# Two layers of cross attention and expert FFNs on one core: column norms between the key products, 16-bit integers in the token lists, two operations moved to other engines

## The chip, the core and the metric

One Trainium2 chip, one of its cores. A core has TensorE (PE; its weight loads are shown apart as PEld), VectorE (DVE), ScalarE (ACT), GpSimd (POOL) and SyncE (SP, which issues DMAs here). The metric is the time of one execution on the device, in microseconds (us); lower is better.

## The reference, cut to what matters

Eight batches of 256 tokens of width 256, so 2048 tokens, go through four blocks, each added to its input after a layer norm. The change touches the first two blocks, and one bound that is worked out in them for the third.

```python
def _L0_xattn_ref(Q, K, V, Wq, bq, Wout, bout):          # block 1
    q = (Q @ Wq + bq).transpose(0, 2, 1)                 # width 16; K and V alike
    ...
    corr = jnp.real(jnp.fft.ifft(Qf * jnp.conj(Kf))).mean(axis=(0, 1))
    W_topk, I_topk = jax.lax.top_k(corr, K_TOP)          # 12 shifts
    W_topk = jax.nn.softmax(W_topk)
    ...                                                  # R: weighted rolls of v
    return R @ Wout + bout

def balanced_assignment(scores):                         # block 2
    for e in range(E):                                   # 8 experts, 256 tokens each
        s = jnp.where(taken, -jnp.inf, scores[:, e])
        _, idx = jax.lax.top_k(s, C)
        parts.append(idx)
        taken = taken.at[idx].set(True)
    return jnp.concatenate(parts)

def _L0_ffn_ref(x, centroids, ln_g, ln_b, w1, b1, w2, b2):
    scores = layer_norm(feat, ln_g, ln_b) @ centroids.T
    sort_by_expert = balanced_assignment(scores)
    routed = feat[sort_by_expert].reshape(E, C, D)
    h = layer_norm(routed, ln_g, ln_b)
    h = jax.nn.gelu(jnp.einsum('ecd,edf->ecf', h, w1) + b1[:, None, :])
    h = jnp.einsum('ecf,efd->ecd', h, w2) + b2[:, None, :]
    out = routed + h                                     # and back to token order

x = x + _L0_xattn_ref(_layernorm(x), ctx, ctx, ...)
x = x + _L0_ffn_ref(_layernorm(x), ...)
x = x + _L1_xattn_ref(_layernorm(x), ctx, ...)           # softmax attention, 16 heads
x = x + _L1_ffn_ref(_layernorm(x), ...)                  # top 2 of 8 gated experts, and shared ones
```

## The kernel before, in words

`fast_path` does all four blocks; `general_path` follows only where a flag says that a bound was broken. The order of instructions on each engine is written out by hand, and each engine executes its instructions in that order. What touches the change lies in the first 170 us:

1. Tokens and context are loaded, transposed and projected. The correlation of block 1 goes through memory (`Gd`, then `DG`), its maximum is taken (`pcorr`, L1757), the weights go through memory (`Wd`, then `CW`, L1787), and three short products follow: `pr3` (L1915), `pp` (L1927), and `PB`, which is spread to all tokens (`spread_rows`, L1850) on top of the tokens' own rows (`copy_rows`, L1836). Statistics of the sums, factors, and the scores `SC` follow up to 57 us.
2. While TensorE waits in this chain it is given steps of other work. `work` is a queue of such steps, and `fill(us)` takes steps from it until their written costs reach `us`; a step of 0.43 is one 128 x 256 product. First in the queue are the keys and values of block 3 (`keys`, L1391, and `vals`, L1412), which need nothing from block 1.
3. `column_norms` (L1374) sums the squares of the columns of Wq of block 3, four products with an output of one column; ACT scales them and POOL takes the root. They stand in slot 4 of the PSUM tile `pw`, among `small_products` (L1869, outputs of 32 columns).
4. Block 2 finds for each expert e a threshold with `search` (five rounds, L2198 to L2230: DVE counts tokens above a value, TensorE adds the counts up in `pcn`, L2215, DVE sets the next value). During the search for expert e the generator `list_tokens(e - 1)` is taken one step on after each round: `taken` and `sel` on DVE (L2253, L2257), `pse` on TensorE (L2262), `selt` and `before` on DVE, `ppl` on TensorE, `place`, `ab`, `oab`, `ob` on DVE (L2291 to L2300), `pid` (L2304) and `pix` (L2312) on TensorE, the token numbers `ids`, and two gathers of the tokens' rows `R` by POOL (L2323).
5. `ffn(e)` starts when the rows are there: ACT applies the layer norm (`R`, L2365), TensorE transposes (`turn_rows`, `prt`, L2385), ACT scales into `RT` (L2389), and 16 steps of `up` (`ph`, then a Gelu on ACT) and 16 of `down` (`py`, L2419) are appended to `work`. After each eight `down` steps DVE adds the bias `b2b` to `py` (L2428) and POOL scatters the 128 rows `Y` to memory (L2429). For experts 2, 3 and 4 `ffn` also copies a column of `blank` on ACT (L2374), and SP then stores blank rows to `Td` (L2376); the next expert's weights are loaded by SP too (L1813 to L1817).
6. SP's queue around 57 us is: the rows' stores to `NMd` (L2018, L2001), `SCd` (L2173), two loads of score rows (L2165), the stores of the factors (L1939), four more score rows, then the blanks `Yd` (L2178) and `Od` (L2182). The gathers of expert 0 need the rows and the factors in `NMd`.

Of the kernel before, what the change touches and what calls it, by code (L numbers as in the profile page):

```python
# [9 lines left out]
F32 = mybir.dt.float32  # L10
BF16 = mybir.dt.bfloat16
U32 = mybir.dt.uint32
I32 = mybir.dt.int32
AF = mybir.ActivationFunctionType
ALU = mybir.AluOpType
# [4 lines left out]
P = 128  # L20
# [1066 lines left out]
def fast_path(  # L1087
# [49 lines left out]
    NTB = T // TB  # L1137
    HW = 32
    F16 = mybir.dt.float16
    assert L0_xattn_Wq.shape[1] == DH and L1_ffn_w1_e.shape[2] == F  # L1140

    def tok_view(ap):
# [36 lines left out]
    def fill(us):  # L1179

        while work and us > 0.3:
            cost, do = work.popleft()
            do()
            us -= cost
# [185 lines left out]
    def column_norms(pn):  # L1370

        for c in range(NB):
            for kc in range(KC):
                nc.tensor.matmul(  # L1374
                    pn[:, c : c + 1],
                    wsq[:, kc, c * P : (c + 1) * P],
                    ones[:, 0:1],
                    start=(kc == 0),
                    stop=(kc == KC - 1),
                )  # L1380
        nc.scalar.activation(qmax, pn, AF.Copy, scale=257.0)
        nc.gpsimd.tensor_tensor(
            qmax, qmax, powers[:, 1:2].to_broadcast([P, NB]), ALU.pow
        )
        nc.gpsimd.tensor_tensor(qmax, qmax, babs, ALU.add)
# [230 lines left out]

    first = pr.tile([P, 4], BF16, name="first")
    nc.gpsimd.tensor_copy(first, ident.rearrange("p (g i) -> p g i", i=32)[:, :, 0])
    identb = pr.tile([P, P], BF16, name="identb")
    nc.gpsimd.tensor_copy(identb, ident)  # L1620
    onesb = pr.tile([P, P], BF16, name="onesb")
# [11 lines left out]
        channel_multiplier=-1,  # L1633
    )

    iab = pr.tile([P, NT, 2, 16], I32, name="iab")
    for j, base in enumerate((BASE // 16, 0)):
        nc.gpsimd.iota(
            iab[:, :, j, :],
# [103 lines left out]
    nc.tensor.transpose(pb1, b1r, ident[: E * NF, : E * NF])  # L1743
    b1c = pr.tile([P, E, NF], F32, name="b1c")
    nc.scalar.copy(b1c.rearrange("p e f -> p (e f)"), pb1)
    fill(4.3)
    nc.vector.scalar_tensor_tensor(tri, identb, float(BASE), tri, ALU.mult, ALU.add)
    ith = pa.tile([P, 1], F32, name="ith")
    nc.vector.tensor_reduce(ith, i32, AX.X, ALU.add)
# [84 lines left out]
    def copy_rows(b, pool, tag):  # L1834
        pos[b] = pool.tile([P, TPB, D], F32, tag=tag, name="po")
        nc.tensor.matmul(  # L1836
            pos[b].rearrange("p h d -> p (h d)"),
            ident,
            rows_of(b).rearrange("p h d -> p (h d)"),
            start=True,  # L1840
            stop=False,
            skip_group_check=True,
        )
# [17 lines left out]
    bdiag = pa.tile([E, E], F32, name="bdiag")  # L1861
    nc.vector.tensor_scalar(bdiag, ident[:E, :E], bnd, None, ALU.mult)
    WCn = pa.tile([P, 3, 32], F32, name="WCn")
    pw = ps_t.tile([P, 5, 32], F32, tag="pt", name="pw")
    pb = pw[:, 3, 0:E]

    def small_products(j):
        for dc in range(KC):
            nc.tensor.matmul(  # L1869
                pw[:, j, :],  # L1870
                wrt[:, dc, j * P : (j + 1) * P]
                if j < 2
                else boc[:, dc : dc + 1].to_broadcast([P, P]),
                cenP[:, dc, :],
                start=(dc == 0),
                stop=(dc == KC - 1),
            )

    copy_rows(order_b[0], ps_t, "pt")
    copy_rows(order_b[1], ps_t, "pt")  # L1880
    small_products(0)
    small_products(1)
    column_norms(pw[:, 4, 0:NB])
    copy_rows(order_b[2], ps_t, "pt")
    small_products(2)
    nc.tensor.matmul(pb, ones[:E, :], bdiag, start=True, stop=True)
    nc.vector.tensor_copy(WCn, pw[:, 0:3, :])
# [354 lines left out]
    def list_tokens(e, then):  # L2242

        if e == E - 1:

            sel = pm.tile([P, TB], BF16, tag="sel", name="sel")
            nc.vector.tensor_scalar(
                sel, taken[e - 1], -1.0, 1.0, ALU.mult, ALU.add
            )
        else:  # L2250
            n, thr = low[e]
            taken.append(pm.tile([P, TB], BF16, tag="taken", name="taken"))
            nc.vector.tensor_scalar(taken[e], n, thr, None, ALU.is_gt)  # L2253
            sel = taken[e]
            if e:
                sel = pm.tile([P, TB], BF16, tag="sel", name="sel")
                nc.vector.tensor_tensor(sel, taken[e], taken[e - 1], ALU.subtract)  # L2257
        yield

        pse = ps_t.tile([P, 4, 4], F32, tag="pt", name="pse")  # L2260
        for j in range(4):
            nc.tensor.matmul(  # L2262
                pse[:, j, :], sel[:, j * P : (j + 1) * P], first, start=True, stop=True
            )
        selt = pm.tile([P, NT], BF16, tag="selt", name="selt")
        nc.vector.tensor_scalar(
            selt.rearrange("p (g j) -> p j g", j=4),
            pse,
            1.0,
            None,  # L2270
            ALU.mult,
            ALU.add,
            accum_out=cnts[:, e : e + 1],
        )
        before = pm.tile([P, NT], BF16, tag="before", name="before")
        nc.vector.memset(before[:, 0:1], 0.0)
        nc.vector.tensor_tensor_scan(
            before[:, 1:],
            onesb[:, 0 : NT - 1],
            selt[:, 0 : NT - 1],  # L2280
            0.0,
            ALU.mult,
            ALU.add,
        )
        yield

        ppl = ps_t.tile([P, NT], F32, tag="pt", name="ppl")
        nc.tensor.matmul(ppl, tri, selt, start=True, stop=False)
        nc.tensor.matmul(ppl, onesb, before, start=False, stop=True)
        place = pm.tile([P, NT], I32, tag="place", name="place")  # L2290
        nc.vector.tensor_copy(place, ppl)  # L2291
        ab = pm.tile([P, NT, 2], I32, tag="ab", name="ab")
        nc.vector.tensor_scalar(ab[:, :, 0], place, 4, None, ALU.logical_shift_right)
        nc.vector.tensor_scalar(ab[:, :, 1], place, 15, None, ALU.bitwise_and)
        oab = pm.tile([P, NT, 2, 16], F16, tag="oab", name="oab")
        nc.vector.tensor_tensor(
            oab, ab.unsqueeze(3).to_broadcast([P, NT, 2, 16]), iab, ALU.is_equal
        )
        ob = pm.tile([P, NT, 16], F16, tag="ob", name="ob")
        nc.vector.tensor_tensor(ob, oab[:, :, 1, :], tok, ALU.mult)  # L2300
        yield
        pid = ps_t.tile([16, 16], F32, tag="pt", name="pid")
        for c in range(NT):
            nc.tensor.matmul(  # L2304
                pid, oab[:, c, 0, :], ob[:, c, :], start=(c == 0), stop=(c == NT - 1)
            )
        ids16 = pm.tile([16, 16], F16, tag="ids16", name="ids16")
        nc.vector.tensor_copy(ids16, pid)
        yield
        pix = ps_t.tile([P, NCT, 16], F32, tag="pt", name="pix")  # L2310
        for r in range(NCT):
            nc.tensor.matmul(  # L2312
                pix[:, r, :], rowsel[:, r, :], ids16, start=True, stop=True
            )
        m = pm.tile([P, NCT, 16], F32, tag="m", name="m")
        nc.vector.tensor_tensor(m, pix, bsel, ALU.mult)
        idf = pm.tile([P, NCT], F32, tag="idf", name="idf")
        nc.vector.tensor_reduce(idf, m, AX.X, ALU.add)
        ids = pm.tile([P, NCT], U32, tag="ids", name="ids", bufs=4)
        nc.vector.tensor_copy(ids, idf)  # L2320
        R = pf.tile([P, NCT, D + 2], F32, tag="R", name="R")
        for r in range(NCT):
            nc.gpsimd.indirect_dma_start(  # L2323
                out=R[:, r, :],
                out_offset=None,
                in_=NMd,
                in_offset=bass.IndirectOffsetOnAxis(ap=ids[:, r : r + 1], axis=0),
            )
        then(e, ids, R)
        if e == E - 1:  # L2330
            for r in range(NCT):
                nc.vector.tensor_scalar(
                    at0[:, r, :], row0, idf[:, r : r + 1], None, ALU.is_equal
                )
# [23 lines left out]
    def ffn(e, ids, R):  # L2358
# [57 lines left out]
        def down(r):  # L2416
            py = ps_k.tile([P, D], F32, tag="pm", name="py")
            for f in range(NF):
                nc.tensor.matmul(  # L2419
                    py,  # L2420
                    A[:, f, r * P : (r + 1) * P],
                    w2[:, f, :],
                    start=(f == 0),
                    stop=(f == NF - 1),
                )
                if f < NF - 1:
                    yield
            nc.vector.tensor_tensor(Y[:, r, :], py, b2b, ALU.add)  # L2428
            nc.gpsimd.indirect_dma_start(  # L2429
                out=Yd,  # L2430
                out_offset=bass.IndirectOffsetOnAxis(ap=ids[:, r : r + 1], axis=0),
                in_=Y[:, r, :],
                in_offset=None,
            )
            yield
# [1048 lines left out]
```

## Time and profile before

| what | us |
|---|---|
| median of 3 runs | 883.61 (883.28 to 885.3) |
| the profiled execution's own time | 878.66 |
| its span, first to last instruction | 876.9 |
| mean granted TensorE clock in it | 0.997 |
| DVE busy from 75 to 105 us of the span | 24.35 of 30 |
| ACT busy from 75 to 105 us | 14.70 of 30 |
| GpSimd busy from 75 to 105 us | 3.88 of 30 |
| TensorE busy from 105 to 155 us | 50.00 of 50 |

The profile's page gives busy time per engine and groups of instructions; the views by time (the timeline, and busy time by stretch) give each instruction's start in us from the span's start. A matmul on 32-bit data appears as two records, each with its own weight load; records overlap, so what one costs TensorE is the distance from its start to the next one's start, not its duration. "[1.38 <-DVE ob L2300]" behind a line says that the engine stood idle for 1.38 us before it, and what ended that.

### The profile page before, as it was taken

The numbers are of one execution on the slowest core, as the hardware profiler recorded it, in microseconds if no ns is written. First come the engines' busy times: TensorE is split into PE (matmuls) and PEld (weight loads), VectorE is DVE, ScalarE is ACT, GpSimd is POOL, SyncE is SP. The second block draws the span as 40 slices with busy tenths as digits, with TensorE's granted clock in tenths as the row PEclk, the third lists the DMA queues.
The fourth block names the chain that finished last, engine by engine and source line by source line (L and its number), as shares of the span: only waits on it lengthen the run. The fifth ranks groups of instructions, "written<-read, shape, count | busy, mean of one in ns | idle before, by whom it ended". The sixth has DMA issues, their size and how long they took to land. (4 is left out here: it accounts for less than half of the span.)

```text
span 876.9 us, 11147 instructions
## 1 busy us (share of the span) xinstructions
PE 856.0 (98%) x4180; PEld 533.7 (61%) x4180; DVE 308.8 (35%) x1017; ACT 266.2 (30%) x494; POOL 213.8 (24%) x298
## 2 busy tenths in 40 slices
PE   8999899999999999999999999999999999999997
PEld 6646688788455555545568474747464657474745
DVE  7377876412656765551111112020111111111021
ACT  4254443332677675321110111111111111111110
POOL 7161222302235464423310020201111131111200
PEclk9999999999999999999999999999999999999999
DMA  8475479840610001361211555565657434311130
GB/s 250 160 223 172 144 210 279 261 130 37 164 42 26 1 20 38 113 237 44 68 50 38 179 141 148 159 177 156 181 155 181 149 92 114 85 13 12 18 103 28
DMA packets 87126, 105.22 MB, mean 120 GB/s; under 512 B 8824, under 2 KB 77656, under 8 KB 87032
## 3 DMA queue, kind: packets, MB, share of 16 engines
q1 hardware_dynamic: 78520, 91.10, 32.9%
q0 software_dynamic: 7920, 13.02, 7.0%
q8 instruction: 35, 0.57, 0.3%
q10 hardware_dynamic: 624, 0.30, 0.1%
q14 instruction: 27, 0.22, 0.1%
HBM read 80.60 MB, written 25.37 MB: 121 GB/s over the span
## 5 line engine op out<-in xcount | busy, mean ns | idle before, releaser
L3113 DVE TENSOR_TENSOR A<-A,pu 128x512 f32<-128x512 f32 x96 | 66.0, 688 | 365.2 <-PE pu L3104 358.5
L3112 ACT ACTIVATE A<-pgt 128x512 f32<-128x512 f32 x96 | 57.3, 597 | 271.5 <-PE pgt L3104 271.5
L3173 POOL DMA_INDIRECT Od<-Y,ids x32 | 49.4, 1545 | 304.0 <-ACT Y L3186 213.3
L3104 PE MATMUL pgt<-RT,wa 128*128 128x512 f32 x256 | 121.2, 596 | 0.0
L3104 PE MATMUL pu<-RT,wb 128*128 128x512 f32 x256 | 120.3, 592 | 0.0
L3126 PE MATMUL py<-wc,A 128*128 128x256 f32 x512 | 111.8, 379 | 0.0
L3126 PEld LDWEIGHTS py<-wc,A 128*128 128x128 f32 x512 | 96.9, 190 | 13.1 <-issue 0.5
L3104 PEld LDWEIGHTS pu<-RT,wb 128*128 128x128 f32 x256 | 48.7, 190 | 61.1 <-issue 59.9
L2689 ACT ACTIVATE ex<-p,scale 128x512 f32<-128x512 f32 x128 | 77.2, 689 | 27.5 <-PE p L2681 26.3
L3104 PEld LDWEIGHTS pgt<-RT,wa 128*128 128x128 f32 x256 | 47.7, 190 | 54.8 <-issue 54.4
L2402 PE MATMUL ph<-RT,w 128*128 128x256 f32 x256 | 61.6, 390 | 1.5 <-ACT RT L2389 1.3
L2419 PE MATMUL py<-w,A 128*128 128x256 f32 x256 | 62.0, 389 | 0.0
L2402 PEld LDWEIGHTS ph<-RT,w 128*128 128x128 f32 x256 | 45.4, 190 | 9.9 <-ACT RT L2389 1.8
L2419 PEld LDWEIGHTS py<-w,A 128*128 128x128 f32 x256 | 46.6, 190 | 6.3
L2921 POOL DMA_INDIRECT Td<-HP,to x32 | 31.6, 988 | 63.3 <-DMA Td<-HP,to 60.3
L2411 ACT ACTIVATE A<-ph,b1c 128x256 f32<-128x256 f32 x64 | 30.0, 472 | 54.4 <-PE ph L2402 51.0
L3104 PE MATMUL pgt<-HT,wa_-1_2734 128*128 128x512 f32 x96 | 45.5, 597 | 0.0
L3104 PE MATMUL pu<-HT,wb_-1_2735 128*128 128x512 f32 x96 | 45.1, 593 | 0.0
L3186 ACT ACTIVATE Y<-py,R 128x256 f32<-128x256 f32 x32 | 15.2, 474 | 96.5 <-PE py L3126 96.5
L2681 PE MATMUL p<-QM,KT 32*128 32x512 f32 x256 | 43.4, 640 | 0.4 <-DVE QM L2662 0.4
L3126 PE MATMUL py<-wc_-1_2736,A 128*128 128x256 f32 x192 | 41.9, 379 | 0.0
L3126 PEld LDWEIGHTS py<-wc_-1_2736,A 128*128 128x128 f32 x192 | 36.5, 190 | 5.7 <-issue 1.0
(458 smaller groups left out, 984.8 us busy)
## 6 DMA issues: line engine op xcount, KB each, us to landing
w<-in_L_ffn_w_dram SPq DMA_DIRECT2D x16, 1024.0 KB, 7.3
wa<-in_L_ffn_w_e_dram SPq DMA_DIRECT2D x8, 1024.0 KB, 7.0
wb<-in_L_ffn_w_e_dram SPq DMA_DIRECT2D x8, 1024.0 KB, 8.7
wc<-in_L_ffn_w_e_dram SPq DMA_DIRECT2D x8, 1024.0 KB, 8.3
R<-Td SPq DMA_DIRECT2D x8, 530.0 KB, 7.2
sa<-in_L_ffn_w_e_dram SPq DMA_DIRECT2D x16, 256.0 KB, 4.2
sb<-in_L_ffn_w_e_dram SPq DMA_DIRECT2D x16, 256.0 KB, 4.8
sc<-in_L_ffn_w_e_dram SPq DMA_DIRECT2D x16, 256.0 KB, 5.7
```

What stands on the lines that cost most here:

```text
L2402: nc.tensor.matmul(ph, w1[:, kc, f * P : (f + 1) * P], RT[:, kc, :], start=(kc == 0), stop=(kc == KC - 1),)
L2411: nc.scalar.activation(A[:, f, :], ph, AF.Gelu_apprx_tanh, bias=b1c[:, e, f : f + 1])
L2419: nc.tensor.matmul(py, A[:, f, r * P : (r + 1) * P], w2[:, f, :], start=(f == 0), stop=(f == NF - 1),)
L2681: nc.tensor.matmul(ps[g].rearrange("p m q -> p (m q)"), KT[rows, c, k0 : k0 + P], QM[b][rows, c].rearrange("p m q -> p (m q)"), start=True ...
L2689: nc.scalar.activation(e4[:, g], ps[g], AF.Exp, scale=scale)
L2921: nc.gpsimd.indirect_dma_start(out=Td, out_offset=bass.IndirectOffsetOnAxis(ap=to[g][:, k, j : j + 1], axis=0), in_=HP[:, GT * g + j, :], ...
L3104: nc.tensor.matmul(ps, w_[:, kc, fs], xs[kc], start=(kc == 0), stop=(kc == KC - 1),)
L3112: nc.scalar.activation(a, pgt, AF.Silu)
L3113: nc.vector.tensor_tensor(a, a, pu, ALU.mult)
L3126: nc.tensor.matmul(py, A[:, f, s : s + P], wc[:, f, :], start=(f == 0), stop=(f == NF - 1))
L3173: nc.gpsimd.indirect_dma_start(out=Od, out_offset=bass.IndirectOffsetOnAxis(ap=ids, axis=0), in_=Y, in_offset=None, compute_op=ALU.add,)
L3186: nc.scalar.activation(Y, py, AF.Copy, scale=R[:, i, D + e : D + e + 1])
```

## The change

`column_norms` moves from between `small_products(1)` and the third `copy_rows` to the middle of the fill before `pcorr`, with a PSUM tile of its own; that fill is written as two of 1.73 instead of one of 4.3, and a fill of 0.86 stands after the third `copy_rows`. `small_products(0)` moves ahead of the second `copy_rows`. The integers `place`, `ab` and the constants `iab` become 16 bits wide. For experts 1, 2 and 3 the difference `sel` is no longer formed by DVE: `pse` adds the product of `taken[e]` with `first` and that of `taken[e - 1]` with its negative `nfirst` (a new constant made by POOL). For experts 0, 1 and 2 the bias is added in two operations, a copy out of PSUM by ACT and an addition by POOL, instead of one by DVE.

```diff
--- before.py
+++ after.py
@@ -1137,6 +1137,7 @@
     NTB = T // TB
     HW = 32
     F16 = mybir.dt.float16
+    I16 = mybir.dt.int16
     assert L0_xattn_Wq.shape[1] == DH and L1_ffn_w1_e.shape[2] == F
 
     def tok_view(ap):
@@ -1616,6 +1617,8 @@
 
     first = pr.tile([P, 4], BF16, name="first")
     nc.gpsimd.tensor_copy(first, ident.rearrange("p (g i) -> p g i", i=32)[:, :, 0])
+    nfirst = pr.tile([P, 4], BF16, name="nfirst")
+    nc.gpsimd.tensor_scalar(nfirst, first, -1.0, None, ALU.mult)
     identb = pr.tile([P, P], BF16, name="identb")
     nc.gpsimd.tensor_copy(identb, ident)
     onesb = pr.tile([P, P], BF16, name="onesb")
@@ -1633,7 +1636,7 @@
         channel_multiplier=-1,
     )
 
-    iab = pr.tile([P, NT, 2, 16], I32, name="iab")
+    iab = pr.tile([P, NT, 2, 16], I16, name="iab")
     for j, base in enumerate((BASE // 16, 0)):
         nc.gpsimd.iota(
             iab[:, :, j, :],
@@ -1743,7 +1746,9 @@
     nc.tensor.transpose(pb1, b1r, ident[: E * NF, : E * NF])
     b1c = pr.tile([P, E, NF], F32, name="b1c")
     nc.scalar.copy(b1c.rearrange("p e f -> p (e f)"), pb1)
-    fill(4.3)
+    fill(1.73)
+    column_norms(ps_t.tile([P, NB], F32, tag="pt", name="pn"))
+    fill(1.73)
     nc.vector.scalar_tensor_tensor(tri, identb, float(BASE), tri, ALU.mult, ALU.add)
     ith = pa.tile([P, 1], F32, name="ith")
     nc.vector.tensor_reduce(ith, i32, AX.X, ALU.add)
@@ -1861,7 +1866,7 @@
     bdiag = pa.tile([E, E], F32, name="bdiag")
     nc.vector.tensor_scalar(bdiag, ident[:E, :E], bnd, None, ALU.mult)
     WCn = pa.tile([P, 3, 32], F32, name="WCn")
-    pw = ps_t.tile([P, 5, 32], F32, tag="pt", name="pw")
+    pw = ps_t.tile([P, 4, 32], F32, tag="pt", name="pw")
     pb = pw[:, 3, 0:E]
 
     def small_products(j):
@@ -1877,11 +1882,11 @@
             )
 
     copy_rows(order_b[0], ps_t, "pt")
+    small_products(0)
     copy_rows(order_b[1], ps_t, "pt")
-    small_products(0)
     small_products(1)
-    column_norms(pw[:, 4, 0:NB])
     copy_rows(order_b[2], ps_t, "pt")
+    fill(0.86)
     small_products(2)
     nc.tensor.matmul(pb, ones[:E, :], bdiag, start=True, stop=True)
     nc.vector.tensor_copy(WCn, pw[:, 0:3, :])
@@ -2252,16 +2257,29 @@
             taken.append(pm.tile([P, TB], BF16, tag="taken", name="taken"))
             nc.vector.tensor_scalar(taken[e], n, thr, None, ALU.is_gt)
             sel = taken[e]
-            if e:
+            if e > 3:
                 sel = pm.tile([P, TB], BF16, tag="sel", name="sel")
                 nc.vector.tensor_tensor(sel, taken[e], taken[e - 1], ALU.subtract)
         yield
 
         pse = ps_t.tile([P, 4, 4], F32, tag="pt", name="pse")
+        less = taken[e - 1] if 0 < e <= 3 else None
         for j in range(4):
             nc.tensor.matmul(
-                pse[:, j, :], sel[:, j * P : (j + 1) * P], first, start=True, stop=True
-            )
+                pse[:, j, :],
+                sel[:, j * P : (j + 1) * P],
+                first,
+                start=True,
+                stop=less is None,
+            )
+            if less is not None:
+                nc.tensor.matmul(
+                    pse[:, j, :],
+                    less[:, j * P : (j + 1) * P],
+                    nfirst,
+                    start=False,
+                    stop=True,
+                )
         selt = pm.tile([P, NT], BF16, tag="selt", name="selt")
         nc.vector.tensor_scalar(
             selt.rearrange("p (g j) -> p j g", j=4),
@@ -2287,9 +2305,9 @@
         ppl = ps_t.tile([P, NT], F32, tag="pt", name="ppl")
         nc.tensor.matmul(ppl, tri, selt, start=True, stop=False)
         nc.tensor.matmul(ppl, onesb, before, start=False, stop=True)
-        place = pm.tile([P, NT], I32, tag="place", name="place")
+        place = pm.tile([P, NT], I16, tag="place", name="place")
         nc.vector.tensor_copy(place, ppl)
-        ab = pm.tile([P, NT, 2], I32, tag="ab", name="ab")
+        ab = pm.tile([P, NT, 2], I16, tag="ab", name="ab")
         nc.vector.tensor_scalar(ab[:, :, 0], place, 4, None, ALU.logical_shift_right)
         nc.vector.tensor_scalar(ab[:, :, 1], place, 15, None, ALU.bitwise_and)
         oab = pm.tile([P, NT, 2, 16], F16, tag="oab", name="oab")
@@ -2425,7 +2443,11 @@
                 )
                 if f < NF - 1:
                     yield
-            nc.vector.tensor_tensor(Y[:, r, :], py, b2b, ALU.add)
+            if e < 3:
+                nc.scalar.copy(Y[:, r, :], py)
+                nc.gpsimd.tensor_tensor(Y[:, r, :], Y[:, r, :], b2b, ALU.add)
+            else:
+                nc.vector.tensor_tensor(Y[:, r, :], py, b2b, ALU.add)
             nc.gpsimd.indirect_dma_start(
                 out=Yd,
                 out_offset=bass.IndirectOffsetOnAxis(ap=ids[:, r : r + 1], axis=0),
```

## The prediction, made before the changed kernel was run

> **What bounds the kernel now.** I read the page's busy times first, then busy time by stretch, the timelines of TensorE and DVE in the stretches that the change touches, and last the waits of SP.
>
> ```profile
> PE 856.0 (98%) x4180; PEld 533.7 (61%) x4180; DVE 308.8 (35%) x1017; ACT 266.2 (30%) x494; POOL 213.8 (24%) x298
> ```
>
> TensorE is the bound; other engines count only where TensorE waits for them, or where its clock is low. All that the change can give back lies in such places before 160 us. The first is in the stretches (PE, PEld, DVE, ACT, POOL busy, then the granted clock, DMA share, GB/s):
>
> ```profile
> 31.60:35.00 3.40, 3.40 (x23) 1.30 (x16) 2.24 (x12) 1.96 (x3) 0.00 (x0) 1.00 0.22 76
> 35.00:38.40 3.40, 3.40 (x25) 2.86 (x25) 0.05 (x1) 0.17 (x1) 1.30 (x4) 1.00 0.54 135
> 38.40:41.80 3.40, 3.40 (x11) 2.37 (x11) 1.71 (x11) 0.00 (x0) 0.00 (x0) 0.50 1.02 383
> 41.80:45.20 3.40, 3.40 (x16) 1.46 (x15) 0.96 (x3) 0.40 (x3) 0.00 (x0) 0.99 1.03 283
> ```
>
> For 3.4 us the clock is halved. The timeline shows what TensorE did before and during it:
>
> ```profile
> 34.76 0.97 PE L1869 MATMUL pw<-cenP,wrt 128*128 128x32 f32 x8
> 35.57 1.03 PE L1374 MATMUL pw<-ones,wsq 128*128 128x1 f32 x8
> 36.46 1.10 PE L1836 MATMUL po<-X,ident 128*128 128x512 f32 x2
> 37.41 0.53 PE L1869 MATMUL pw<-cenP,boc 128*128 128x32 f32 x4
> ...
> 38.17 1.88 PE L1915 MATMUL pr<-vT,CW 128*128 128x128 f32 x8
> 39.84 1.91 PE L1836 MATMUL po<-X,ident 128*128 128x512 f32 x2
> 41.55 1.17 PE L1927 MATMUL pp<-wout,R 128*128 128x256 f32 x4
> ```
>
> A 512-column record takes 0.43 us (36.46 to 37.31), so 0.03 us of a 32-column one's 0.11 us streams columns, and almost none of a 1-column one's. Of 35.0 to 38.4 only some 1.4 us (0.85 for the copy, 0.25 for `pr3`, the rest small) does: products that keep PE "busy" come just ahead of the half clock. The second place is the search for expert 3, where the queue of work is empty:
>
> ```profile
> 94.81 0.24 PE L2262 MATMUL pse<-first,sel 128*128 128x4 bf16 x4
> ...
> 96.24 0.19 PE L2215 MATMUL pcn<-B32h,cnt 128*128 128x32 f16 x1 [0.21 <-DVE above L2198]
> ...
> 98.23 0.18 PE L2215 MATMUL pcn<-B32h,cnt 128*128 128x32 f16 x1
> 99.78 0.56 PE L2304 MATMUL pid<-ob,oab 128*16 128x16 f16 x16 [1.38 <-DVE ob L2300]
> 100.27 0.66 PE L2385 MATMUL prt<-ident,R 128*128 128x128 f32 x4
> 101.58 0.70 PE L2402 MATMUL ph<-RT,w 128*128 128x256 f32 x2 [0.65 <-ACT RT L2389]
> ```
>
> Two other stalls wait on transfers: 79 us (expert 0's rows) and 158 us (expert 5's).
>
> **Column norms and fills (term A).** The clock first. At full clock the eight `pr3` records take 8 x 0.11 = 0.88 instead of 1.67 (38.17 to 39.84), the two copy records 0.85 instead of 1.71; `pp` then starts at 39.90 instead of 41.55 and ends at 40.95 instead of 42.72, so `PB` and all behind it move 1.77 earlier. R3 on DVE (0.36 wait + 0.48) fits under the copy: 39.22 + 0.84 = 40.06, which costs 0.16 of that; I take 1.6. After the change the worst 3.4 us near there hold about 0.9 us of sparse products between dense copies and keys, so I expect no half clock; the bound is 0 if it stays.
>
> Not all arrives. The stall at 79 us ends when expert 0's rows land, and that hangs on SP's queue: `SCd` is stored at 57.35, the score loads wait for it, the factors' stores stand behind them, and the gathers (71.96) behind those.
>
> ```profile
> SPq L2165 <- DMA SCd<-SC: 2.9, 1, 2.9
> ```
>
> DMA is full from 36 to 58 us (share 1.02), so the rows' stores end no earlier, and `SCd`, queued behind them, gains part of 1.6. From issue of that store to the next issue takes 57.35 to 60.77, 3.4 us; the store of `Wd`, as large and with free queues, took 33.32 to 35.45, 2.1. If the rows end when they did, `SCd` gains no more than the 1.3 between, perhaps nothing. I take -0.7, bounds 0 and -1.6; what TensorE saves beyond it lengthens the stall at 79 us.
>
> [...]
>
> Work is conserved: 4.3 took ten steps, two 1.73 take four each, 0.86 two. Ahead of `pcorr` two steps (0.87) make room for the norms (35.57 to 36.46, 0.89) and two switches of kind (a first record after a small one shows 0.30 for 0.22): +0.1, which delays the chain and then returns behind `pr3`. Bounds 0 and +0.2. The root (0.70) and sum (0.20) on POOL fall into its idle 10.6 us before L1382, ACT's 0.17 between key copies; uncovered, that copy's 0.17. `nfirst` costs what `first` does, 0.19 on POOL; it has 1.27 idle before L1754 soon after, else +0.19.
>
> **16-bit integers (term B).** On DVE these rows bear on the change (out<-in, count, busy, mean ns):
>
> ```profile
> L2296 DVE TENSOR_TENSOR oab<-ab,iab 128x512 f16<-128x512 int32 x8 | 5.5, 692 | 0.3
> L2428 DVE TENSOR_TENSOR Y<-py,b2b 128x256 f32<-128x256 f32 x8 | 3.4, 421 | 1.4 <-PE py L2419 1.4
> L2257 DVE TENSOR_TENSOR sel<-taken 128x512 bf16<-128x512 bf16 x6 | 2.6, 426 | 0.2
> ```
>
> `oab` has 512 elements at 692 ns, `sel` as many 16-bit ones at 426: the gain is 0 or 0.27 for each list. Only expert 2's (98.71) lies on a path; the other seven have TensorE busy or transfers waited for. `ab` is one element repeated 16 times, unlike `sel`'s dense operands; the nearest row of the same reading is `oab` itself, so I take 0, bounds -0.27 and 0. The conversions have 16 elements (170 ns) and keep their cost.
>
> [...]
>
> **Differences and outputs (terms C, D).** DVE loses 3 x 0.43 (`sel`) and 6 x 0.42 (`Y`), 3.8 in all; what counts is from 92 to 102 us. There `sel` (94.27) and `Y` (94.61) stand between `taken` and the count `few` at 94.95, which moves to 94.28; `pcn` cannot follow, since TensorE still has eight records to do, and goes at 95.95 instead of 96.24; the next `few` 96.20 instead of 96.76; the second `pcn` 97.90; `ob` ends 0.58 earlier, so `pid` at 99.20. Behind it the new order on ACT shows: both copies of expert 0's `py` come ahead of the two `R` operations of expert 1 (0.60 each), which ran at 95.42 without them. The second copy waits for `py`, 98.03 + 0.37, then two `R`, 0.57 apart: 99.57, `prt` to 100.2, `RT`, and `ph` at 101.0 instead of 101.58. C is -0.55; bounds: 0 if ACT's order eats it, -1.27 if all three operations count.
>
> Term D: four more `pse` matmuls cost 0.11 (94.81 to 94.92, four) for each of three experts; expert 2's is inside C, so +0.22, bounds 0 and +0.33. POOL's addition should take what its 128x256 `SC` addition did, 0.72; each scatter goes about 0.7 later, and the gathers behind have idle time: 1.98 before 133.96, 2.89 before 119.07. Without it expert 4's rows would be late by up to 0.7. ACT has 15 of 30 us idle from 75 to 105.
>
> **Sum.** -0.7 + 0.1 + 0 - 0.55 + 0.22 = -0.93. The profiled execution takes 878.66 (span 876.9 and 1.76 around it), so its successor 877.7; the median of the runs is 883.61, 4.95 more, which this profile does not explain. I apply the difference to it: 882.7.
>
> **Rivals.**
>
> *Everything arrives.* DMA follows the chain whole (-1.6), all three DVE operations count (-1.27), and `oab` runs like `sel` (-0.27): with +0.32 that is -2.8, 880.8. For it: nothing but fullness by share says that stores can't end earlier. Against: `pcn` has TensorE work ahead of it.
>
> *Nothing arrives.* `SCd` lands when it did (0), ACT's order eats C (0), +0.32 remains: 883.9. For it: the stall at 79 us ends by a transfer; against: 1.3 of `SCd`'s 3.4 us is queueing.
>
> *Slower: blank rows behind ACT.* Expert 1's first `Y` copy (113.1, as `py` ends) comes ahead of expert 2's `R` (111.00 before) and of the copy of `blank` at 112.0, for which SP waits with `Td` and the next weights behind it. They go some 2.5 later, into expert 3's gathers (119.07, 5.9 to landing, against 3.1 for expert 2's). Rows landing at 126.3 leave 4.2 to `prt` at 130.52; two `R` need 1.2, so it decides from 3.0 late, then us for us. If the gathers end behind all 2.6 MB (8.9 us at 296 GB/s from 114.7) and 1 MB more (3.5), plus 3.1, they land at 130.2: 0.9 stall, and with the 0.32 and no gain 884.8. Against: gathers share, not queue.
>
> **How the numbers follow.** Forecast 882.7, 0.60, own range 881.4 to 883.7. Everything 0.24, nothing 0.09, slower 0.07. Range 880.3 to 884.5: the low side takes in the first rival, the high side the last two. A measurement here tells some 0.3%, 2.65 us, from no change: below 880.96 is faster, 0.22 (most of the first rival); above 886.26 slower, 0.06, a slower rival at two experts; same 0.72.
>
> **What would show it.** Right: clock 1.00 from 35 to 45 us, `PB` near 41.3; the stall at 79 us longer; `oab` at 690 ns; expert 1's `R` after 98; `pid` some 0.6 closer to the `prt` of expert 0; no stall from 105 to 155 us. Wrong: a half clock elsewhere, `oab` near 430, gathers of experts 2 to 4 late, or a stall of TensorE for ACT after its new copies.

## The result, and the profile after

| | before | after |
|---|---|---|
| median of 12 executions each | 883.86 us | 883.64 us |
| ratio after to before, with its 95% interval | | 0.9996 (0.9985 to 1.0006) |
| the profiled execution's own time, span | 878.66, 876.9 | 882.9, 881.2 |
| mean granted clock in it | 0.997 | 0.994 |

No difference that can be told from none. The two profiled executions do differ, by 4.3 us of span, and 0.003 of clock over 880 us is, as an estimate from these two figures, 2.6 of these. So the two traces must be compared piece by piece, and the clock kept apart. First the busy time by stretch of the kernel after, with the stretches of before's dip first and then those of the stall on expert 0's rows and of the search for expert 3 (columns: stretch, length, busy time of PE, PEld, DVE, ACT, POOL, granted clock, DMA share, GB/s):

```profile
35.00:38.40 3.40, 3.40 (x18) 2.48 (x16) 0.00 (x0) 0.47 (x1) 0.00 (x0) 1.00 0.54 148
38.40:41.80 3.40, 3.33 (x17) 2.25 (x16) 1.99 (x12) 0.00 (x0) 0.00 (x0) 1.00 1.02 386
...
78.40:81.80 3.40, 0.88 (x4) 0.41 (x4) 0.43 (x2) 2.02 (x5) 0.00 (x0) 1.00 0.89 314
81.80:85.20 3.40, 3.08 (x14) 2.17 (x14) 1.47 (x7) 1.54 (x4) 0.00 (x0) 0.56 0.35 127
99.00:102.50 3.50, 1.98 (x26) 1.44 (x24) 3.26 (x14) 1.85 (x4) 1.23 (x2) 1.00 0.27 87
102.50:105.90 3.40, 2.75 (x13) 1.88 (x10) 1.41 (x8) 1.02 (x2) 0.60 (x1) 0.53 1.02 333
105.90:109.30 3.40, 3.40 (x11) 2.09 (x10) 1.43 (x6) 1.43 (x3) 0.44 (x1) 0.50 0.05 12
```

The half clock at 38.4 us is gone; three stretches of it stand at 82 and from 103 to 109 us, where before had none. Each is 3.41 us long, at a granted clock of 0.50. By an estimate from these two numbers, at most half of that, some 1.7 us of TensorE's work, is lost in each.

What became of the time saved at 38 us is told by SP's queue. Its timeline, first of before, then of after (start, duration, line, out<-in):

```profile
57.35 0.33 SPq L2173 DMA_DIRECT2D SCd<-SC  x1
60.77 1.27 SPq L2165 DMA_DIRECT2D row<-SCd  x2
```

```profile
56.11 0.33 SPq L2178 DMA_DIRECT2D SCd<-SC  x1
60.95 1.28 SPq L2170 DMA_DIRECT2D row<-SCd  x2
```

The scores are stored 1.24 us earlier and the loads that wait for that store are issued 0.18 later. Everything behind them follows: the gathers go at 72.41 instead of 71.96, and TensorE, which comes to the stall 1.24 earlier, only waits longer in it. Its pauses there sum to 4.05 us, against 2.12, counted from a record's start to the next one's start, less the usual distance; the idle times in the lines below sum to 3.56 and 1.64. Its timeline in the stall, before and after:

```profile
77.38 1.54 PE L1412 MATMUL pp<-wkv_in,CT 128*128 128x256 f32 x6
79.36 0.44 PE L2385 MATMUL prt<-ident,R 128*128 128x128 f32 x2 [0.44 <-ACT R L2365]
80.33 0.44 PE L2385 MATMUL prt<-ident,R 128*128 128x128 f32 x2 [0.54 <-ACT R L2365]
81.43 0.70 PE L2402 MATMUL ph<-RT,w 128*128 128x256 f32 x2 [0.66 <-ACT RT L2389]
```

```profile
76.14 1.54 PE L1413 MATMUL pp<-wkv_in,CT 128*128 128x256 f32 x6
79.27 0.44 PE L2403 MATMUL prt<-ident,R 128*128 128x128 f32 x2 [1.58 <-ACT R L2383]
81.03 0.44 PE L2403 MATMUL prt<-ident,R 128*128 128x128 f32 x2 [1.32 <-ACT R L2383]
82.12 1.16 PE L2420 MATMUL ph<-RT,w 128*128 128x256 f32 x2 [0.66 <-ACT RT L2407]
```

The records of `ph` last 1.16 and not 0.70: the half clock has begun. The last place is the list of expert 2, on three engines of the kernel after:

```profile
100.33 0.18 PE L2220 MATMUL pcn<-B32h,cnt 128*128 128x32 f16 x1
102.03 0.56 PE L2322 MATMUL pid<-ob,oab 128*16 128x16 f16 x16 [1.52 <-DVE ob L2318]
```

```profile
100.55 0.69 DVE L2314 TENSOR_TENSOR oab<-ab,iab 128x512 f16<-128x512 int16 x1
101.28 0.70 DVE L2318 TENSOR_TENSOR ob<-oab,tok 128x256 f16<-128x256 f16 x1
```

```profile
100.99 0.83 POOL L2448 TENSOR_TENSOR Y<-Y,b2b 128x256 f32<-128x256 f32 x1 [2.11 <-ACT Y L2447]
```

`oab` on 16-bit integers takes what it did on 32-bit ones (693 and 692 ns). `ob` takes 0.70 us here and 0.29 in the seven other lists; this is the one list in which GpSimd's new addition runs beside it. From `pcn` to `pid` it is 1.70 us, against 1.55 before (98.23 to 99.78).

### The profile page after: what moved, and what is told of

It is laid out like the page before. It is cut to its first block, busy times and chain, and to the rows that moved or that the text cites. A ratio compares the mean times of both kernels' runs of the same rounds, so it can differ in the third digit from the quotient of the medians.

```text
span 881.2 us, 11174 instructions
## 1 busy us (share of the span) xinstructions
PE 860.3 (98%) x4192; PEld 536.3 (61%) x4192; DVE 307.6 (35%) x1008; ACT 268.3 (30%) x500; POOL 218.6 (25%) x305
## 5 line engine op out<-in xcount | busy, mean ns | idle before, releaser
L2420 PE MATMUL ph<-RT,w 128*128 128x256 f32 x256 | 66.0, 407 | 1.5 <-ACT RT L2407 1.3
L2420 PEld LDWEIGHTS ph<-RT,w 128*128 128x128 f32 x256 | 47.5, 200 | 11.0 <-ACT RT L2407 1.9
```

Source lines behind the costliest of these rows:

```text
L2420: nc.tensor.matmul(ph, w1[:, kc, f * P : (f + 1) * P], RT[:, kc, :], start=(kc == 0), stop=(kc == KC - 1),)
```

## The experiments

The runs were made on two chips, with the kernel before run beside them on the same chip: its medians were 884.72 (35 executions), 884.8 (29) and 883.67 (17), so only ratios are compared across groups. "Mean clock" is that of all timed executions of a kernel. Over before's 35, the time falls by 0.92 us for each 0.001 of clock.

This table is of the profiled executions: when `SCd` was stored and when the loads behind it went, the first transpose of expert 0's rows, the distance from `pcn` to expert 2's `pid`, and the half clock in the first 300 us (every profile has a last stretch of it at its end).

| kernel | SCd | row loads | prt | pcn to pid | half clock, us | ratio (95%) |
|---|---|---|---|---|---|---|
| before | 57.35 | 60.77 | 79.36 | 1.55 | 3.4 | 1 |
| after | 56.11 | 60.95 | 79.27 | 1.70 | 10.2 | 0.9996 (0.9985 to 1.0006) |
| e1_norms | 55.93 | 61.95 | 80.20 | 1.56 | 6.8 | 1.0003 (0.9984 to 1.0023) |
| e2_diff | 56.11 | 61.47 | 80.14 | 1.38 | 10.2 | 0.9993 (0.9976 to 1.0011) |
| e3_out | 55.80 | 61.18 | 79.57 | 1.96 | 13.7 | 1.0022 (1.0009 to 1.0035) |
| e4_int16 | 56.01 | 62.19 | 80.77 | 1.56 | 6.8 | 0.9989 (0.9972 to 1.0006) |
| e9_no_out | 56.11 | 62.84 | 81.51 | 1.39 | 3.4 | 0.9988 (0.9973 to 1.0004) |
| e10_dve_add | 55.81 | 61.84 | 80.62 | 1.56 | 13.7 | 1.0018 (1.0001 to 1.0035) |
| e6_blanks | 55.81 | 61.77 | 80.58 | 1.69 | 13.7 | 1.0004 (0.9986 to 1.0023) |
| e5_weights | 55.95 | 58.09 | 77.37 | 1.70 | 3.4 | 0.9934 (0.9912 to 0.9957) |
| e7_both | 56.00 | 58.14 | 77.41 | 1.69 | 3.4 | 0.9949 (0.9933 to 0.9965) |
| e11_before_w | 55.92 | 58.06 | 77.33 | 1.55 | 3.4 | 0.9924 (0.9906 to 0.9941) |
| e12_abc_w | 55.77 | 57.91 | 77.18 | 1.38 | 3.4 | 0.9927 (0.9904 to 0.9949) |
| e13_busy | 56.01 | 58.16 | 77.44 | 1.54 | 0 | 0.9927 (0.9908 to 0.9945) |

**The parts one at a time, on the kernel before.** Column norms and fills alone:

```diff
-    fill(4.3)
+    fill(1.73)
+    column_norms(ps_t.tile([P, NB], F32, tag="pt", name="pn"))
+    fill(1.73)
...
+    small_products(0)
     copy_rows(order_b[1], ps_t, "pt")
-    small_products(0)
     small_products(1)
-    column_norms(pw[:, 4, 0:NB])
     copy_rows(order_b[2], ps_t, "pt")
+    fill(0.86)
```

> The kernel before with the column norms and fills of the change alone. Theory H (held): the chain moves about 1.2 us earlier, SCd is stored near 56.1 instead of 57.35, but the first score load still goes out at 60.5 to 61, expert 0's second row block still lands at 79.5 to 80.5, TensorE's gaps between the key and value products and the first ph add up to some 3.3 to 4 us instead of 2.1, and the median is within 0.6 us of before. Rival P (passed on): the 1.2 us reaches the end and another part of the change loses it; then the median is 1.0 to 1.5 us below before. Rival C (clock by chance): the half clock stays at 38 us in this profile too.

Nothing is gained that can be told; the interval, from 1.4 us below before to 2.0 above, leaves room for theory P too. The trace speaks for H: `SCd` goes at 55.93, but the row loads behind it at 61.95, later even than H had them. The pauses of the stall (to `prt`, to the second half of the rows, to `ph`) sum to 5.4 us by the same count, more than H gave.

The differences in TensorE alone (a `nfirst` of GpSimd is added; the four products with it take the place of `sel`):

```diff
-            if e:
+            if e > 3:
                 sel = pm.tile([P, TB], BF16, tag="sel", name="sel")
...
+                nc.tensor.matmul(
+                    pse[:, j, :],
+                    less[:, j * P : (j + 1) * P],
+                    nfirst,
...
```

> The kernel before with the differences of experts 1 to 3 formed in TensorE alone. Theory: in the search for expert 3 pid comes 0.2 to 0.4 us earlier after prt of expert 0 than before (19.45 us there), eight pse matmuls take 0.22 us instead of 0.11; the median is within 0.4 us of before. Rival: the twelve matmuls more are all paid and nothing is won, +0.3 us.

`pcn` to `pid` shrinks from 1.55 to 1.38, and the 0.21 us that TensorE waited before the first `pcn` of that search is gone. Eight `pse` records take 0.20. The whole is within the uncertainty. The sign by the distance from expert 0's `prt` to `pid` can't be read, here or in the next run: 6.8 us of half clock lie in it, from 81.9 and from 80.8 us on.

The outputs by ACT and GpSimd alone:

```diff
-            nc.vector.tensor_tensor(Y[:, r, :], py, b2b, ALU.add)
+            if e < 3:
+                nc.scalar.copy(Y[:, r, :], py)
+                nc.gpsimd.tensor_tensor(Y[:, r, :], Y[:, r, :], b2b, ALU.add)
+            else:
+                nc.vector.tensor_tensor(Y[:, r, :], py, b2b, ALU.add)
```

> The kernel before with the outputs of experts 0 to 2 by ScalarE and GpSimd alone. Theory S (shared): what DVE saves (2 x 0.42 us before pid of the search for expert 3) is given back where GpSimd's addition runs beside a 16-bit DVE operation: ob takes 0.6 to 0.8 us instead of 0.29 where they meet, pid comes at most 0.3 us earlier after expert 0's first prt than before (20.42 us there); median within 0.4 us of before. Rival O (order): the R operations of experts 1 and 2, now behind the Y copies on ScalarE, and SP's blank stores behind them cost 1 us or more.

The one part that costs. All twelve executions ran at a clock of 0.991 or 0.992, against a mean of 0.9934 of before. By the 0.92 us above, 0.0020 of clock is worth 1.8 us, as much as the difference of the medians (1.74): the lower clock accounts for all of this cost that can be told. Its DVE and its GpSimd in expert 2's list:

```profile
102.40 0.69 DVE L2296 TENSOR_TENSOR oab<-ab,iab 128x512 f16<-128x512 int32 x1
103.13 0.69 DVE L2300 TENSOR_TENSOR ob<-oab,tok 128x256 f16<-128x256 f16 x1
```

```profile
102.58 1.10 POOL L2430 TENSOR_TENSOR Y<-Y,b2b 128x256 f32<-128x256 f32 x1 [2.22 <-ACT Y L2429]
```

GpSimd's addition takes 1.10 where the kernel after shows 0.71 to 0.83 for it, and it ends (103.68) shortly before `ob` does (103.82). `oab`, which the addition meets from 102.58 on, keeps its 0.69; `ob` takes 0.69 where it takes 0.29 in other lists. So, side by side, the addition took 0.36 us longer than its median in the kernel after (0.74), and `ob` 0.40 longer; what makes them longer isn't shown.

The 16-bit integers alone:

```diff
-    iab = pr.tile([P, NT, 2, 16], I32, name="iab")
+    iab = pr.tile([P, NT, 2, 16], I16, name="iab")
...
-        place = pm.tile([P, NT], I32, tag="place", name="place")
+        place = pm.tile([P, NT], I16, tag="place", name="place")
```

> The kernel before with 16-bit place, ab and iab alone. Theory: oab stays at 0.69 us, place and ab at 0.17 to 0.18 us, the median is within 0.3 us of before. Rival: oab falls to about 0.43 us as dense 16-bit operands do, and pid of the search for expert 3 comes 0.27 us earlier.

Here `oab` has a median of 693 ns, and `pcn` to `pid` stays at 1.56.

One thing all four show together. e2_diff, e3_out and e4_int16 keep the old order around the column norms, yet none has the half clock at 38 us, and `SCd` goes at 55.8 to 56.1 in them as in the rest. So before's dip there, which one of five profiles with the old order shows, isn't in every execution. The other four (with e11_before_w below) add up `PB` at 41.2 to 41.5 us, as the nine profiles with the new order do; only before's profile, with the dip, has it at 42.76. Whether the new order rules the dip out, or only missed it in nine profiles, isn't shown.

**What holds the transfer.** Two suspects stand ahead of the gathers. The first is expert 1's weights, 2 MB loaded from 37.5 us on, ahead of the rows' stores:

```diff
-    W0 = {e: load_l0(e) for e in range(2)}
+    W0 = {0: load_l0(0)}
...
     nc.sync.dma_start(out=Od[T:, :], in_=blank[:, 0:D])
+    W0[1] = load_l0(1)
```

> The changed kernel, with expert 1's weights (2.1 MB) loaded after the blank stores instead of ahead of the rows' stores. Theory H (the rows' stores hold SCd back): the wait of the first score load for SCd falls from 4.3 us to 2.0 to 2.6, the gathers of expert 0 go out 2 to 3 us earlier than 72.4 and 73.95, TensorE's stall behind the key and value products (4.05 us with the change) falls to about 2, and the median is 1.5 to 3.5 us below before. Rival B (blanks): the gathers go out earlier, but the Yd store goes out earlier with them and they land no sooner than 79.5; the median stays within 0.8 us of before.

The second is the stores of blank rows, which run beside the gathers. In the next kernel they are moved behind expert 0's rows:

```diff
-    nc.sync.dma_start(
-        out=Yd.rearrange("(c p) d -> p c d", p=P),
...
+            if e == 0 and r == NCT - 1:
+                nc.scalar.copy(blank[:, 0:1], blank[:, 1:2])
+                nc.sync.dma_start(
+                    out=Yd.rearrange("(c p) d -> p c d", p=P),
...
```

> The changed kernel, with the blank stores to Yd and Od issued after expert 0's rows have landed (ScalarE rewrites a column of zeros behind its R operations, SP waits for that). Theory B (the 2 MB store slows the gather): the gathers go out as with the change (72 to 74) and take 3 to 4 us to land instead of 6.0 and 6.4, the stall falls from 4.05 to about 2 us, the median is 1.5 to 3.5 us below before. Rival H: landing stays near 6 us, the median within 0.8 us of before.

And both edits at once, with the weights behind the moved stores:

> The changed kernel with both edits: blanks, then expert 1's weights, behind the landing of expert 0's rows. If H and B both hold: second row block landed before 77, stall under 1.5 us, no half clock between 75 and 95 us, median 3 to 5 us below before. If only one holds, the median is that of its own run.

The weights are the cause; moving the blank stores bought nothing on its own, and nothing on top. With the blanks out of the way the gathers of expert 0 still took 6.5 to 6.6 us to land (6.0 and 6.4 in the kernel after). Moving the weights gained 6.1 us, more than the 1.5 to 3.5 of the theory. With the weights away the wait of SP is the bare store and load, from 3.4 to 6.7 us down to 2.1, in each of the five kernels that have the move. Then the move on the kernel before, without any of the change:

> The kernel before, with nothing of the change, but expert 1's weights are loaded after the stores of blank rows instead of at the start of the expert stage. Theory: the queue behind which the score rows' store stands holds the stall at 79 us in every version, so the move alone brings most of the gain: the wait of SP for that store falls from about 3 to 4 us to 1.6, expert 0's rows land 2 to 3 us earlier, ratio 0.993 to 0.996. If the change itself brings what was forecast for it once the transfer is free (0.9 us), this run is 0.5 to 1.5 us slower than the changed kernel with the same move (ratio 0.9934). Rival: the gain of the move belongs to the change's own earlier chain, and alone it brings at most 0.2%.

The move alone brings all of it, ratio 0.9924, and it isn't the 0.5 to 1.5 us slower than e5_weights (0.9934) that it would be if the change brought its 0.9 us once the transfer is free. The busy time by stretch where `SCd` is stored, before and here (DMA share is the last figure but one):

```profile
52.00:55.40 3.40, 2.47 (x42) 1.09 (x36) 1.88 (x12) 1.29 (x3) 2.03 (x2) 1.00 1.12 271
55.40:58.80 3.40, 3.37 (x21) 2.16 (x15) 2.97 (x10) 1.65 (x4) 1.85 (x7) 1.00 1.00 249
```

```profile
52.00:55.40 3.40, 2.48 (x31) 1.49 (x27) 2.57 (x12) 1.43 (x4) 0.83 (x2) 1.00 0.32 88
55.40:58.80 3.40, 3.37 (x16) 2.39 (x16) 3.01 (x14) 1.43 (x4) 2.80 (x11) 1.00 0.20 77
```

The store no longer meets a full DMA (share 0.32 and 0.20, against 1.12 and 1.00). Of the 6.1 us between the medians (883.67 and 877.58) the clock accounts for 3.6, as its mean rose from 0.9939 to 0.9978 (3.9 x 0.92). The rest, 2.5, is left for the shorter stall itself; no run parts the two.

**The outputs again.** The changed kernel with the outputs on DVE as before (the diff of e3_out taken back):

> The changed kernel with all outputs added by DVE again (norms, integers and differences stay). Theory: the outputs on GpSimd cost some 1.5 to 2 us by two windows of half clock near 103 to 110; without them that half clock is there in few executions, the mean clock of the timed runs rises from 0.993 to 0.994 or 0.995, and the median is 1 to 2 us below before. Rival: the other parts gain nothing either, the median is within 0.5 us of before.

And with ACT's copy kept, but the addition on DVE:

```diff
                 nc.scalar.copy(Y[:, r, :], py)
-                nc.gpsimd.tensor_tensor(Y[:, r, :], Y[:, r, :], b2b, ALU.add)
+                nc.vector.tensor_tensor(Y[:, r, :], Y[:, r, :], b2b, ALU.add)
```

> The changed kernel, but for experts 0 to 2 DVE and not GpSimd adds the bias to the output that ACT has copied. It tells apart two causes for what the outputs on their own cost (ratio 1.0022). Theory N, the two additions of GpSimd collide with DVE's product ob: in the profile ob of expert 2's list takes 0.29 us and not 0.70, expert 2's differences go to TensorE some 0.4 us earlier after the stall, and the time is 1 to 1.5 us below the changed kernel's, ratio 0.997 to 0.999. Rival A, ACT's order (its copies of the output ahead of expert 1's gain and bias) is what costs: ob is short, but TensorE's wait before the first product of expert 1's hidden layer stays as it was, and the ratio stays at 1.000 to 1.002.

e9_no_out leaves 1.39 from `pcn` to `pid`, and its time, 1.1 us below before at a mean clock of 0.9942, goes the way of its theory but can't be told from no change. e10_dve_add has `ob` at 0.29 and 1.56. So the collision is real, 0.41 us of `ob`, but e10_dve_add isn't the faster for its absence: 1.0018. That half of the theory fell. The signs that the rival named came true: `ob` is short, the ratio is in its range, and from the last `prt` to the first `ph` of expert 1 it is still 0.93. But it is 0.93 in e9_no_out and in before too, which have no copies on ACT, so this wait isn't where an ACT copy costs. What it costs beyond the collision stays open.

**Everything but the outputs, with the weights later**, and then the same with TensorE kept busy in the pauses:

```diff
+    def keep_busy(n):
+        for _ in range(n):
+            nc.tensor.matmul(pdum, ones, ones, start=True, stop=True)
...
+        if e == 2:
+            keep_busy(6)
         pid = ps_t.tile([16, 16], F32, tag="pt", name="pid")
...
+            if e < 2:
+                keep_busy(3)
```

> The norms, the 16-bit integers and the differences of the change, the outputs left on DVE as before, and expert 1's weights loaded later. Theory: the outputs on ACT and GpSimd are the one part that costs, so without them the time is 0.5 to 1.5 us below the changed kernel with the move: ratio 0.991 to 0.994, and the product ob takes 0.29 us in the profile. Rival: once the transfer is freed the stall before expert 2's differences is what is left, and DVE's six additions in its way cost as much as the collision did: ratio 0.993 to 0.995.

> As the run before this one, with 15 more or so products of a 128x128 tile of ones with itself (six ahead of expert 2's differences, three after the transposes for each of experts 0 and 1) that go to a bank of their own and into nothing of the output. They are work added. Theory H, the half clock near 80 to 110 us comes of the pauses of TensorE in the stalls there: with the pauses filled the mean granted clock rises to 0.998 or more and the time falls by 1 to 1.7 us against the run before it, ratio 0.990 to 0.992. [...]

e12_abc_w (877.3) can't be told from e11_before_w (877.58): with the transfer freed the change without its outputs still adds nothing. With its outputs, in e5_weights, the ratio is 0.9934, so the 0.5 to 1.5 us that the outputs were to cost can't be told there either. In e13_busy (12 products are added, the 15 above is a miscount) the clock went the way expected, to a mean of 0.9988 from 0.9977, and its profile has no half clock before the end. But six executions each, at 0.995 to 0.999 and at 0.998 to 1.000, don't make that rise certain, and e12_abc_w's profile had no half clock from 80 to 110 us to begin with. The time didn't fall (877.29): 0.0011 of clock would be worth 1.0 us, which is less than the 1.6 to 2.0 us that the two intervals reach each way, and the products delay `pid` by 0.16 (1.38 to 1.54). So the remedy isn't shown to be one.

What ties the half clock to the pauses is the move of the weights. The dip that begins between 80 and 84 us stands in eight of the nine profiles with the weights in place, all but before's, whose stall was short, and in none of the five in which the move shortened the stall.

What stands ahead of a half clock can be read by cutting the span at multiples of 3.41 us, the length of a dip, from a dip of the same execution: after's dips at 82.22 and 102.70 lie six such lengths apart (20.48 us), and before's at 38.42 and 874.69 lie 245 (836.27 us). The busy time in such stretches; the clock in a line is that of its own stretch, so what followed it shows one line below. Before, where the stall is cut in two:

```profile
75.97:79.38 3.41, 2.97 (x15) 2.02 (x14) 3.08 (x12) 1.26 (x3) 0.00 (x0) 1.00 1.07 386
79.38:82.79 3.41, 2.22 (x11) 1.52 (x12) 1.65 (x9) 2.23 (x6) 0.00 (x0) 1.00 0.77 278
82.79:86.21 3.42, 3.42 (x23) 2.76 (x21) 3.06 (x19) 2.79 (x6) 0.00 (x0) 1.00 0.35 126
```

After:

```profile
75.39:78.81 3.42, 2.29 (x11) 1.41 (x9) 3.16 (x11) 0.57 (x2) 0.00 (x0) 1.00 1.07 382
78.81:82.22 3.41, 0.98 (x5) 0.51 (x5) 0.02 (x1) 2.25 (x6) 0.00 (x0) 1.00 0.79 286
82.22:85.63 3.41, 3.41 (x16) 2.50 (x17) 1.67 (x10) 1.27 (x3) 0.00 (x0) 0.50 0.35 126
99.29:102.70 3.41, 1.89 (x26) 1.45 (x25) 3.20 (x13) 1.85 (x4) 1.43 (x2) 1.00 0.32 98
102.70:106.11 3.41, 2.75 (x9) 1.90 (x9) 1.40 (x9) 1.02 (x2) 0.40 (x1) 0.50 0.98 325
```

e9_no_out, and then e10_dve_add, in the search for expert 3:

```profile
101.00:104.41 3.41, 2.20 (x27) 1.65 (x26) 3.20 (x14) 0.00 (x0) 0.06 (x1) 1.00 0.19 50
104.41:107.83 3.42, 2.77 (x15) 1.95 (x15) 2.54 (x13) 1.98 (x4) 0.92 (x1) 1.00 1.01 336
```

```profile
101.69:105.10 3.41, 2.00 (x25) 1.35 (x24) 3.20 (x14) 1.85 (x4) 0.62 (x1) 1.00 0.31 76
105.10:108.51 3.41, 2.79 (x7) 1.88 (x7) 1.93 (x11) 1.48 (x4) 0.36 (x1) 0.50 0.92 309
```

In these lines a stretch at full clock with 2.20 us of TensorE or more is followed by full clock, and one with 0.98, 1.89 or 2.00 by half; e5_weights has one with 1.48 (96.49 to 99.91) that is followed by half. The stretch at half clock with 2.75 us (102.70) is followed by another one at half clock, the one with 3.41 (82.22) by full clock. Busy time alone doesn't part the two: before's stretches with 2.00 us (157.90) and 2.03 (96.45) were followed by full clock, and its dip at 38 us followed one with 3.42 of sparse products (35.01). So, as an estimate from these lines alone, the place where a stall of a few us falls among such stretches can decide between nothing and 1.7 us or more; and they begin at other times in before (79.38) than in after (78.81).

## Why the prediction was right, and where it wasn't

The time was right: "no change", forecast 882.7, measured 883.64, inside the range and inside the forecast's own range. That says little for the working, as the 0.93 us that it forecast is less than the 2.65 that it said could be told from no change. The working was right in parts only, and by its terms the rival "nothing arrives" (883.9) came nearer. With what the traces show below in place of its terms (A 0, C -0.24, D +0.18, and the +0.1 of the fills, which no run tells apart) the sum is 0.0. So "no change" came true because the forecast gain was too small to be told from none, not because it arrived.

- **Term A, -0.7, is the step that failed.** `SCd` did go earlier (1.24), as the chain of half-clock records had it, and the store that is queued behind the rows did hold it, as the rival said: the row loads gained nothing (-0.18). So A was 0, what the rival "nothing arrives" has for "`SCd` lands when it did", and e1_norms's time, though its interval would allow -0.7, agrees. And in executions without the dip there was less to win from the start: in nine kernels with the new order and four others with the old one `SCd` goes at 55.8 to 56.1, so the 3.41 us of half clock at 38 us weren't there to be won in those four. I took -0.7 from the one profile at hand.
- **The stall at 79 us has a price.** I said it would lengthen and took that as free. Against before's profile it did, from 1.64 to 3.56 us of idle time, and a half clock follows it, which costs up to 1.7 more: the mishap "a half clock elsewhere", named but not priced. But it isn't shown to be the change's doing: e2_diff, e3_out and e4_int16, with the old order, have 4.4, 4.4 and 5.2 us of idle time there and 6.8 us of half clock behind it. The short stall, like the dip at 38 us, belonged to the one execution that I read.
- **Term B, 0: right.** `oab` takes 693 ns on 16-bit integers and took 692 on 32-bit ones, and e4_int16 is within the uncertainty.
- **Term C, -0.55: reached without the outputs, missed with them.** These are distances in the traces; in the times none of it can be told. Counting TensorE's two waits in the search for expert 3 above the normal distance of such records (py to `pcn` 0.59 for 0.21, `pcn` to `pid` 1.55 for 0.03): 0.38 + 1.53 before, 0 + 1.36 in e9_no_out and in e2_diff, which is -0.55, and 0 + 1.67 after, which is -0.24. Freeing DVE of the addition gains some 0.10 by difference; making GpSimd do it costs `ob` 0.41. The forecast gave POOL's addition its duration and idle time, but not what runs beside it on DVE.
- **ACT's order**: expert 1's `R` went at 101.30, behind the copy, as said; expert 2's at 119.42. Neither made TensorE wait: expert 1's `prt` follows `pid` at 102.51 without idle time, and from 109.6 to 155 us it is busy 45.34 of 45.40, and the rival of blank rows behind ACT did not come, though SP did wait 17.9 us there.
- **Term D, +0.22: right.** Eight `pse` records take 0.20 (97.20 to 97.40) where four took 0.11: 0.09 for each of two experts, 0.18.
- **Other signs.** `PB` came at 41.48, as said (41.3). `pid` was to come some 0.6 closer to the `prt` of expert 0; it came 22.76 us behind it instead of 20.42, with the half clock from 82.2 us on in between. And the range's upper end, 884.5, doesn't take in the slower rival's 884.8, though the prediction says that it does.
- **The 4.95 us left unexplained.** The profiled execution of before had a clock of 0.997, the top of the 0.991 to 0.997 of its 35 later ones (mean 0.9934), and a short stall: its row loads went 3.4 us behind `SCd`, where the eight other kernels with the weights in place took 4.8 to 6.7. The clock is worth 3.3 us (3.6 x 0.92), the short stall may be the rest.

## What to carry to other kernels

Read what ends the stall behind a gain before counting the gain: here the store in the way of everything stood behind 2 MB that weren't needed for another 40 us, and moving one load brought some 0.7% where four edits on engines brought none. Take a dip of the clock in one profile, and the length of a stall that waits for a transfer, as properties of that execution until a second one shows them: here both came out otherwise in the three other profiles with the old order and the weights in place. An operation moved to GpSimd is to be laid beside what DVE does at that moment (here an `ob` of 0.29 us took 0.70), not only into GpSimd's own idle time.

## What the runs showed of the hardware that wasn't expected

- In the profiles of before and after the granted clock fell to 0.50 for 3.41 us or twice that, and the dips of one profile began a whole number of 3.41 us apart (six between after's at 82.22 and 102.70, 245 between before's at 38.42 and 874.69). Cut at such places, stretches with 0.98, 1.48, 1.89 and 2.00 us of TensorE were followed by a half clock (after, e5_weights, after, e10_dve_add), and others with 2.00, 2.03 and 2.20 were not (before, before, e9_no_out). One such dip is worth up to 1.7 us by the estimate above, more than any part of the change. The spread of before, 881.6 to 886.8 us in 17 executions, goes along with clocks of 0.991 to 0.996.
- The loads that wait for the store of scores went 2.1 us behind it where the DMA share around it was 0.32 and 0.20 (e11_before_w), and 3.4 us behind it at 1.12 and 1.00 (before). Over the nine kernels with the weights in place it was 3.4 to 6.7 us, a spread of 3 us with the same stores.
- A 128x256 16-bit product of DVE took 0.29 us, and 0.70 beside a GpSimd addition, whose own time went from 0.74 (its median in the kernel after) to 0.83 and 1.10.
